# Moving part of the edge listing from VectorE to GpSimd in a two-layer graph attention kernel

## The chip, the core and the metric

The kernel runs on one core of a Trainium2 chip. The metric is the device time of one execution in microseconds. Three runs of the kernel before gave 1906.88, 1908.4 and 1909.48 us; the median, 1908.4 us, is the time that the prediction starts from. One more execution was recorded by the profiler (span 1902.5 us); all the rows below are from it.

## What is computed

Two graph attention layers over 3327 nodes with 1024 features, each followed by a residual and a normalisation. The adjacency matrix is sparse (each node has some 17 neighbours), symmetric, and has ones on its diagonal. Cut to what matters:

```python
h = (x @ W).reshape(C, H, D)                  # 8 heads of 128
e = alpha_src[:, :, None] + alpha_dst[:, None, :]
e = jnp.where(e >= 0, e, 0.2 * e)
e = jnp.where(adj[None] == 0, -jnp.inf, e)
out = jnp.einsum('hij,hjd->hid', softmax(e), h_heads)
x = layernorm(x + out)                        # layer 0
# layer 1: the same with one head, h = x @ W1, and a relu on the sum
```

## The kernel before

The 3327 rows are 26 tiles of 128 (the last one short). The kernel has two parts.

The **first part** does two jobs at the same time. It projects: `x @ W0` with 347 columns more or less at a time, three cuts of 8 matmuls for each tile (`project`, L475, TensorE row L479; `flip`, L470, transposes x first), and ScalarE brings the sums out of PSUM (`keep`, L485). And it lists edges: for each tile of 128 target rows, the columns of the ones in 128 x 3327 bytes of the adjacency matrix become a list of source rows, `idx`, and of targets, `tgt`. The **second part** (`sparse`, L741) fetches the listed rows by indirect DMA on the GpSimd queue, 17 for each tile and layer, and adds them up with matmuls. It can start only when the flag of L697 is read, for which the last list must have been counted and made.

The list of one tile t takes these steps (class `Edges`, L280 to L450):

- `words` (L301): GpSimd clears the diagonal (L308), ScalarE counts the ones of each row (L311, `junk`, the only large ScalarE step), VectorE folds the bytes into words (L318).
- `ends` and `ends2` (L324, L343): a matmul with a triangle of ones sums the counts up (L327, L346), ScalarE reads it (L328, L347), and GpSimd works out where each row's edges begin and end, in chains of seven and of five operations of one or two elements (L335 to L341, L348 to L353).
- `keys` and `columns` (L355, L364): VectorE finds up to 32 columns of each row by repeated search for the 8 largest (L274) and removal (L276); the result is `pack`, 128 x 32.
- `places` (L379): ScalarE takes the distance of each place from the middle of a row's stretch (L384 for 512 places, L385 for 128 more, `away`); a comparison with the row's count turns this into a 0/1 matrix `place` in bf16 (L391, L392). `pack` is split into a bf16 part and a bf16 remainder and put into `mv`, one of four buffers (L388, L389). `factors` (L291), called from `keep`, puts the exponentials of the source scores into the same kind of buffer on GpSimd (L296 to L299).
- `give` (L394): TensorE multiplies `place` by `mv` (L411, L401), which moves each row's columns to the places of its edges. `take` (L415): ScalarE reads the result out of PSUM into `xs` and others (L423 to L428).
- `sources` (L431): which of the 32 columns a place takes is an offset difference `kq` (L436, L437); an equality with 0 to 31, a product and a sum (L439 to L445) pick it, and `idx` is written (L450).

What sets the order is written out by hand. All engines take their instructions in the order of the program; `listing` (L506) is a generator of 7 steps for each tile, and `pace` (L537), called after every second matmul of the projection, takes the next step when it is due. In a round of it, the tile before (`old`) gives its places, the next tile (`new`) has its keys and columns searched, then come `take`, `count` of the tile four ahead, `sources` of the old tile, and `places` of the new one:

```python
                if old:
                    old.give(EB)
                    old.take()
                count(t + 4)
                yield
                if old:
                    old.sources()
                    yield
                while new and t + 1 not in scored:
                    yield
                if new:
                    new.places()
                    yield
```

The `while` sees to it that the factors of a tile are issued before its places. Since the projection and the list go at different rates, `keep`, with its four GpSimd operations and its ScalarE steps, falls in another place of the round from tile to tile.

Buffers: `pack`, `away`, `kq` and `xs` have one each, `place` has two, `mv` four.

Of the kernel before, what the change touches and what calls it, by code (L numbers as in the profile page):

```python
# [14 lines left out]
OP = mybir.AluOpType  # L15
# [4 lines left out]
P = 128  # L20
# [6 lines left out]
def kernel(  # L27
# [28 lines left out]
    nc = tc.nc  # L56
# [11 lines left out]
    KMAX = 32  # L68
    GT = 32
    NG = P // GT  # L70
    EB = 4
# [9 lines left out]
    NX = KMAX + 2 + H  # L81
    NY = NX + 2
    XO, XL = 1 + H, 2 + H
# [3 lines left out]
    def rows(t):  # L87
        return min(P, N - t * P)
# [68 lines left out]
    class Phase:  # L157
# [10 lines left out]
        def sbuf(self, tag, shape, bufs, name=None, dt=F32):  # L168
            return self.pool.tile(shape, dt, tag=tag, name=name or tag, bufs=bufs)
# [110 lines left out]
    class Edges:  # L280
# [83 lines left out]
        def columns(self, half):  # L364

            sbuf, ph = self.ph.sbuf, self.ph
            if half == 0:
                ki = sbuf("ki", [P, 2, KMAX], 1, dt=I32)
                nc.vector.tensor_copy(ki[:, 0, :], self.top)
                nc.vector.tensor_scalar(ki[:, 1, :], ki[:, 0, :], 511, None, op0=OP.bitwise_and)  # L370
                bits = sbuf("bits", [P, 8, KMAX], 1, dt=I32)
                nc.vector.tensor_tensor(bits, ki[:, 0:1, :].to_broadcast([P, 8, KMAX]), ph.bit, OP.bitwise_and)
                self.cols = sbuf("cols", [P, 8, KMAX], 1)
                nc.vector.tensor_tensor(self.cols, ki[:, 1:2, :].to_broadcast([P, 8, KMAX]), ph.base, OP.add)
                nc.vector.scalar_tensor_tensor(self.cols, bits, 0.0, self.cols, op0=OP.not_equal, op1=OP.mult)
                self.pack = sbuf("pack", [P, KMAX], 1)
            ph.largest(self.pack, self.cols.rearrange("p a b -> p (a b)"), half)

        def places(self):  # L379

            sbuf, ph, pack = self.ph.sbuf, self.ph, self.pack

            away = sbuf("away", [P, (EB + 1) * P], 1)
            nc.scalar.activation(away[:, : EB * P], ph.io_q, AF.Abs, bias=self.mid, scale=-1.0)  # L384
            nc.scalar.activation(away[:, EB * P :], ph.io_q[:, :P], AF.Abs, bias=self.mid2, scale=-1.0)  # L385

            mv = self.mv = ph.mvs[self.t % 4]
            nc.vector.tensor_copy(mv[:, 0, XL:NX], pack)  # L388
            nc.vector.tensor_tensor(mv[:, 1, XL:NX], pack, mv[:, 0, XL:NX], OP.subtract)  # L389
            self.place = sbuf("place", [P, (EB + 1) * P], 2, dt=BF16)  # L390
            nc.vector.tensor_scalar(self.place[:, : EB * P], away[:, : EB * P], self.deg, None, op0=OP.is_lt)  # L391
            nc.vector.tensor_scalar(self.place[:, EB * P :], away[:, EB * P :], self.more, None, op0=OP.is_lt)  # L392

        def give(self, b):  # L394

# [35 lines left out]
        def sources(self):  # L431

            sbuf, ph, t = self.ph.sbuf, self.ph, self.t
            xv, m = self.xs, NB - 1
            kq = sbuf("kq", [P, NB], 1)
            nc.vector.tensor_tensor(kq[:, :m], ph.io_k[:, :m], xv[:, :m, 0], OP.subtract)  # L436
            nc.vector.tensor_tensor(kq[:, m:], ph.io_k[:, m:], xv[:, m, KMAX + 1 :], OP.subtract)  # L437
            eq = sbuf("eq", [P, NB, KMAX], 1)
            nc.vector.tensor_tensor(  # L439
                eq, ph.io_l.unsqueeze(1).to_broadcast([P, NB, KMAX]),  # L440
                kq.unsqueeze(2).to_broadcast([P, NB, KMAX]), OP.is_equal,
            )
            nc.vector.tensor_tensor(eq, eq, xv[:, :, 1 : KMAX + 1], OP.mult)
            v = sbuf("v", [P, 2, NB], 1)
            nc.vector.tensor_reduce(v[:, 0, :], eq, AX.X, OP.add)  # L445

            nc.vector.tensor_scalar(
                v[:, 1, :], v[:, 0, :], 0.0, float(NONE if t > 1 else 1), op0=OP.is_equal, op1=OP.mult
            )
            nc.vector.scalar_tensor_tensor(idx[:, t, :], v[:, 0, :], -1.0, v[:, 1, :], op0=OP.add, op1=OP.add)  # L450


    with ExitStack() as own, tc.manual_schedule():
        ph = Phase(own, "proj", {"A": 2, "S": 1, "T": 2})
# [204 lines left out]
        for t in range(3, NT):  # L659
# [3 lines left out]
            if t == 12:  # L663
                n, own = NT - 1, pool.tile([P, NT], I32, bufs=1, name="own")
                nc.vector.memset(own[:, n:], 0)
                step, m = adj.ap[0][0] + 1, rows(n)
# [563 lines left out]
```

## Time and profile before

| Engine | busy, us | share of the span | instructions |
|---|---|---|---|
| TensorE matmul (PE) | 1502.7 | 79% | 14663 |
| TensorE weight load (PEld) | 887.9 | 47% | 14663 |
| VectorE (DVE) | 1146.0 | 60% | 3058 |
| ScalarE (ACT) | 546.5 | 29% | 1422 |
| GpSimd (POOL) | 1032.3 | 54% | 1391 |

GpSimd's time is nearly all in the second part, where it issues the fetches. In the first part it is busy for 12 or 13 us in 50. How the views are read: in the timeline, a row has the start and the length in us, the engine, the line of the program, what is written and read with its size, and in brackets the idle time before it and what ended that time. In the stretches, each engine's busy time is followed by the number of instructions. In the waits, a row gives the waiting engine and line, what it waited for, the total in us, the number of times, and the longest. In the groups, a row gives the busy time and the mean in ns, and after the next bar the idle time ahead of it. The ends of matmuls are modelled, so a TensorE that looks busy is not at its peak.

### The profile page before, as it was taken

Reading aid. Unit: us, or ns where it says so; the run is one execution under the profiler, and the core shown is the slowest. Engines: PE = TensorE matmul, PEld = TensorE weight load, DVE = VectorE, ACT = ScalarE, POOL = GpSimd, SP = SyncE. Lnnn points to the kernel's source line nnn. Section 1 sums busy time; section 2 is a strip of 40 time slices with the busy share of each in tenths; the row PEclk is TensorE's granted clock in tenths of the full one; section 3 lists DMA queues with packets and bytes.
Section 4 is the critical chain, followed back from the end, with each engine's and each line's share of the span. In section 5 each row is a group of like instructions: output and inputs, shape, how many; then the busy total and the mean of one; then the engine's idle time right before and its main releaser. Section 6 shows DMA issues by size and latency. Waiting matters only on the chain.

```text
span 1902.5 us, 38082 instructions
## 1 busy us (share of the span) xinstructions
PE 1502.7 (79%) x14663; PEld 887.9 (47%) x14663; DVE 1146.0 (60%) x3058; ACT 546.5 (29%) x1422; POOL 1032.3 (54%) x1391
## 2 busy tenths in 40 slices
PE   8699999999366556555556555399999999999997
PEld 5355555566254545445445444144444444444443
DVE  5799999987286666666666666344444444444442
ACT  5554544452123222222222222012222212222220
POOL 3322222220477666676666764577766667666650
PEclk9899999999678788888888888699999999999999
DMA  7656555421799999999999997899999999999980
GB/s 182 88 115 131 111 104 106 87 72 39 276 369 400 400 401 399 376 406 398 390 388 392 398 383 279 325 401 407 403 370 385 380 378 373 354 372 373 365 326 33
DMA packets 171068, 567.76 MB, mean 298 GB/s; under 512 B 27690, under 2 KB 34346, under 8 KB 170878
## 3 DMA queue, kind: packets, MB, share of 16 engines
q0 software_dynamic: 131056, 455.68, 67.2%
q1 hardware_dynamic: 39822, 109.56, 15.3%
q8 instruction: 118, 1.93, 0.4%
q14 instruction: 72, 0.59, 0.1%
HBM read 578.85 MB, written 42.97 MB: 327 GB/s over the span
## 4 chain that ended last, share of the span: by engine, by line
PE 50%; DMA 24%; DVE 12%; ACT 6%; issue 4%; POOL 3%; DVEq 0%; ACTq 0%; SPq 0%; POOLq 0%
DMA src<-h_d,idx 22%; PE mm L1023 20%; PE acc L991 12%; PE mm L479 11%; DVE e L868 3%; ACT junk L311 3%; PE acc L896 2%; PE tr L176 2%; POOL src L801 2%; DVE pr L929 1%; ACT xT L179 1%; DMA wt<-in_L_gnn_W_dram 1%; PE acc L880 1%; DVE top L274 1%; PE xp L411 1%
## 5 line engine op out<-in xcount | busy, mean ns | idle before, releaser
L801 POOL DMA_INDIRECT src<-h_d,idx x416 | 443.3, 1066 | 201.6 <-PE acc L896 52.3
L801 POOL DMA_INDIRECT src<-y_d,idx x416 | 415.4, 999 | 222.1 <-PE acc L991 89.4
L896 PE MATMUL acc<-src,e 128*32 128x128 f32 x6656 | 267.7, 328 | 260.0 <-DVE e L868 259.6
L479 PE MATMUL mm<-wt,xT 128*128 128x347 f32 (+1 forms) x1248 | 402.5, 468 | 3.1 <-DMA wt<-in_L_gnn_W_dram 2.5
L1023 PE MATMUL mm<-wt,xT 128*128 128x512 f32 x832 | 383.3, 604 | 0.8 <-DVE o L1026 0.8
L896 PEld LDWEIGHTS acc<-src,e 128*32 128x32 f32 x6656 | 226.3, 133 | 316.7 <-DVE e L868 290.7
L479 PEld LDWEIGHTS mm<-wt,xT 128*128 128x128 f32 x1248 | 228.2, 192 | 111.2 <-ACT ht L496 6.7
L1023 PEld LDWEIGHTS mm<-wt,xT 128*128 128x128 f32 x832 | 152.2, 190 | 199.5 <-issue 179.1
L991 PE MATMUL acc<-src,es 128*32 128x342 f32 (+1 forms) x2496 | 205.6, 463 | 33.8 <-DVE es L982 30.9
L868 DVE TENSOR_TENSOR e<-oh,way 128x1024 f32<-128x1024 f32 x130 | 158.8, 1221 | 60.6 <-ACT w L866 60.3
L991 PEld LDWEIGHTS acc<-src,es 128*32 128x32 f32 x2496 | 71.5, 111 | 158.8 <-issue 113.1
L866 ACT ACTIVATE w<-way 128x32 f32<-128x32 f32 (+1 forms) x130 | 24.7, 190 | 399.7 <-DVE way L864 388.3
L1026 DVE SCALAR_TENSOR_TENSOR o<-mm,y 128x512 f32<-128x512 f32 x52 | 36.0, 692 | 166.1 <-PE mm L1023 166.1
L1005 ACT ACTIVATE z<-y,ri 128x342 f32<-128x342 f32 (+1 forms) x78 | 39.5, 569 | 313.8 <-DVE ri L1001 313.8
L863 DVE TENSOR_TENSOR way<-src,re 128x32 f32<-128x32 f32 x104 | 20.9, 201 | 171.6 <-DMA src<-h_d,idx 153.2
L179 ACT ACTIVATE xT<-tr 128x512 f32<-128x512 f32 x104 | 59.3, 595 | 150.7 <-PE tr L176 150.7
L979 DVE TENSOR_TENSOR way<-way,src 128x128 f32<-128x128 f32 x104 | 31.1, 299 | 89.9 <-DMA src<-y_d,idx 44.4
L311 ACT ACTIVATE junk<-ad 128x3328 uint8<-128x3328 uint8 x26 | 78.3, 3013 | 16.1 <-POOL ad L308 16.1
L848 ACT ACTIVATE own<-own,es 128x128 f32<-128x128 f32 x208 | 63.6, 388 | 59.7 <-DVE es L845 59.7
L880 PE MATMUL acc<-end,e 128*128 128x128 f32 x416 | 63.0, 313 | 15.3 <-DVE e L868 15.3
L335 POOL TENSOR_TENSOR place_of<-cnt 128x1 f32<-128x1 f32 x26 | 5.0, 191 | 122.1 <-ACT cnt L328 102.5
L296 POOL CAST mvs<-r 128x8 bf16<-128x8 f32 x26 | 6.0, 231 | 118.2 <-ACT r L295 118.2
(188 smaller groups left out, 1953.7 us busy)
## 6 DMA issues: line engine op xcount, KB each, us to landing
h_d<-ht SPq DMA_DIRECT2D x26, 520.0 KB
own<-h_d SPq DMA_DIRECT2D x26, 520.0 KB
y_d<-y SPq DMA_DIRECT2D x26, 514.0 KB
y<-y_d SPq DMA_DIRECT2D x26, 514.0 KB
x<-in_x_dram SPq DMA_DIRECT2D x25, 512.0 KB
y<-in_x_dram SPq DMA_DIRECT2D x25, 512.0 KB
out_dram<-o SPq DMA_DIRECT2D x25, 512.0 KB
ad<-in_adj_dram POOLq DMA_DIRECT2D x25, 415.9 KB
```

The lines of the kernel that those rows point to most:

```text
L176: nc.tensor.transpose(tr[:, k, :], src[:, (4 * g + k) * P : (4 * g + k + 1) * P], ident)
L179: nc.scalar.activation(part, tr, AF.Copy)
L311: nc.scalar.activation(junk, ad, AF.Copy, accum_out=self.deg)
L479: nc.tensor.matmul(acc, xT[t][:, k, :], wt[:, k, CUTS0[c] : CUTS0[c + 1]], start=k == 0, stop=k == KT - 1)
L801: nc.gpsimd.indirect_dma_start(out=s[:, g, :w], out_offset=None, in_=table[:, :], in_offset=bass.IndirectOffsetOnAxis(ap=idx[:, t, b * NG ...
L848: nc.scalar.activation(hn, hn, AF.Copy, scale=es[:, n : n + 1])
L868: nc.vector.tensor_tensor(e, oh.unsqueeze(2).to_broadcast([P, ng, H, wide]), wp.unsqueeze(3).to_broadcast([P, ng, H, wide]), OP.mult,)
L880: nc.tensor.matmul(self.acc[h // 4][:, h % 4, :], e[:, 0, h, :], rowsof[:, 0, h, :], start=False, stop=h % 4 == 3,)
L896: nc.tensor.matmul(self.acc[h // 4][g * GT : (g + 1) * GT, h % 4, :], e[:, g, h, :], rowsof[:, g, h, :], start=first and h % 4 == 0, stop= ...
L991: nc.tensor.matmul(self.acc[c][to, :m], es[:, g, :], s[:, g, CUTS[c] : CUTS[c + 1]], start=b == 0, stop=b == EB,)
L1005: nc.scalar.activation(z[:, cut], self.res[:, cut], AF.Copy, scale=ri[:, 1:2])
L1023: nc.tensor.matmul(acc, xT[:, k, :], wt1[:, k, half], start=k == 0, stop=k == KT - 1)
```

## The change

Six operations for each tile go from VectorE's queue to GpSimd's: the two comparisons that make `place`, the two copies that split `pack`, and the two differences that make `kq`. `pack` gets a second buffer, so that VectorE can write the next tile's columns while GpSimd still reads this one's. It is meant to take work off VectorE, which is nearly always busy in the first part. The order of the program stays as it is on TensorE, ScalarE and the DMA queue of SyncE; the instructions leave one queue and stand at the same point of the program in another.

```diff
@@ columns
-                self.pack = sbuf("pack", [P, KMAX], 1)
+                self.pack = sbuf("pack", [P, KMAX], 2)
@@ places
-            nc.vector.tensor_copy(mv[:, 0, XL:NX], pack)
-            nc.vector.tensor_tensor(mv[:, 1, XL:NX], pack, mv[:, 0, XL:NX], OP.subtract)
+            nc.gpsimd.tensor_copy(mv[:, 0, XL:NX], pack)
+            nc.gpsimd.tensor_tensor(mv[:, 1, XL:NX], pack, mv[:, 0, XL:NX], OP.subtract)
             self.place = sbuf("place", [P, (EB + 1) * P], 2, dt=BF16)
-            nc.vector.tensor_scalar(self.place[:, : EB * P], away[:, : EB * P], self.deg, None, op0=OP.is_lt)
-            nc.vector.tensor_scalar(self.place[:, EB * P :], away[:, EB * P :], self.more, None, op0=OP.is_lt)
+            nc.gpsimd.tensor_scalar(self.place[:, : EB * P], away[:, : EB * P], self.deg, None, op0=OP.is_lt)
+            nc.gpsimd.tensor_scalar(self.place[:, EB * P :], away[:, EB * P :], self.more, None, op0=OP.is_lt)
@@ sources
-            nc.vector.tensor_tensor(kq[:, :m], ph.io_k[:, :m], xv[:, :m, 0], OP.subtract)
-            nc.vector.tensor_tensor(kq[:, m:], ph.io_k[:, m:], xv[:, m, KMAX + 1 :], OP.subtract)
+            nc.gpsimd.tensor_tensor(kq[:, :m], ph.io_k[:, :m], xv[:, :m, 0], OP.subtract)
+            nc.gpsimd.tensor_tensor(kq[:, m:], ph.io_k[:, m:], xv[:, m, KMAX + 1 :], OP.subtract)
```

In GpSimd's queue the two copies stand directly ahead of the two comparisons. In front of them stand, in the order of the program, the diagonal and the mask's DMA issue of `count`, then `kq`, and in some rounds the four factors of `keep`; behind them come the chains of `ends` and `ends2`.

## The prediction

> **What bounds the kernel now.** The page's 40 slices show two parts. In the first 10 slices (to about 488 us) DMA moves 39 to 182 GB/s, against some 400 later, and TensorE is at 9 tenths or more from slice 3 on; this is where the edges are listed and x@W0 is projected, and it is the only part that the diff touches. The second part begins at the flag (L697, 486 us), whose value needs the last list. So what counts is when the first part ends. Second view, busy time by stretch:
>
> ```profile
> core 0: us, PE busy (x) PEld busy (x) DVE busy (x) ACT busy (x) POOL busy (x), PEclk, DMA share, GB/s
> 111.00:160.00 49.00, 46.37 (x316) 28.32 (x314) 43.62 (x125) 24.50 (x66) 11.92 (x54) 1.00 0.60 130
> 160.00:190.00 30.00, 29.78 (x202) 18.21 (x202) 28.28 (x81) 14.57 (x41) 7.95 (x36) 1.00 0.62 126
> 190.00:300.00 110.00, 105.66 (x728) 65.10 (x727) 100.05 (x282) 55.27 (x148) 26.46 (x122) 1.00 0.54 108
> 408.00:481.00 73.00, 73.00 (x495) 44.57 (x494) 54.65 (x152) 22.11 (x74) 8.72 (x42) 1.00 0.11 41
> ```
>
> VectorE (DVE) is 89 to 94% busy, which invites unloading it. But TensorE is 95 to 100% busy, and its own work (624 projection matmuls, the flips, the places) is unchanged: the part can shorten only by TensorE's idle time. Third view, the waits, TensorE in 78:481 and VectorE in 100:440:
>
> ```profile
> PE xp L411 <- DVE place L391: 20.6, 15, 9.7
> DVE place L391 <- ACT away L384: 11.4, 17, 1.5
> ```
>
> TensorE's idle time is the wait of the first L411 of a list for `place`; 9.7 of the 20.6 us is list 0 (TensorE starved at 68 to 78 us while ScalarE counts three masks). So 10.9 us is the most that could be won later. And in 17 of 22 lists VectorE itself stood waiting for ScalarE's `away`. Fourth view, the timeline of list 20:
>
> ```profile
> 385.71 0.22 PE L401 MATMUL xp<-mvs,place 128*128 128x43 bf16 x3
> 386.92 3.02 ACT L311 ACTIVATE junk<-ad 128x3328 uint8<-128x3328 uint8 x1
> 390.36 0.21 ACT L295 ACTIVATE r<-sd 128x8 f32<-128x8 f32 x1
> 390.59 0.45 ACT L496 ACTIVATE ht<-mm 128x330 f32<-128x330 f32 x1
> 390.92 0.73 ACT L384 ACTIVATE away<-io_q,place_of 128x512 f32<-128x512 f32 x1
> 391.46 0.21 POOL L299 TENSOR_TENSOR mvs<-r,mvs 128x8 bf16<-128x8 f32 x1
> 391.68 0.49 DVE L391 TENSOR_SCALAR place<-away,cnt 128x512 bf16<-128x512 f32 x1 [0.68 <-ACT away L384]
> 392.23 0.24 PE L411 MATMUL xp<-mvs,place 32*128 32x42 bf16 x12 [0.36 <-DVE place L391]
> ```
>
> The loop is TensorE (L401 of the list before) -> ScalarE (xs, the 3.02 us count, ht, away) -> place -> TensorE. `place` starts 0.03 us after `away` ends; VectorE's load is not in it. Setting `away`, `place` and L411 side by side for the 26 lists: `place` was late because of VectorE only in lists 6, 7, 15, 16 and 18. List 15:
>
> ```profile
> 313.13 0.71 ACT L384 ACTIVATE away<-io_q,place_of 128x512 f32<-128x512 f32 x1
> 314.76 0.48 DVE L391 TENSOR_SCALAR place<-away,cnt 128x512 bf16<-128x512 f32 x1
> 315.30 0.24 PE L411 MATMUL xp<-mvs,place 32*128 32x42 bf16 x12 [0.76 <-DVE place L391]
> ```
>
> [...] The trace [...] has no one-input compare. [...] GpSimd's L348 takes 0.19 us 21 times and 0.40 to 0.42 us five times.
>
> **The change, part by part.** It takes off VectorE per list, from these rows (100:440): 0.179 + 0.192 + 0.516 + 0.280 + 0.181 + 0.152 = 1.50 us of some 14.2 us, 39 us in all:
>
> ```profile
> L391 DVE TENSOR_SCALAR place<-away,cnt 128x512 bf16<-128x512 f32 x22 | 11.4, 516 | 11.4 <-ACT away L384 11.4
> L392 DVE TENSOR_SCALAR place<-away,place_of 128x128 bf16<-128x128 f32 x21 | 5.9, 280 | 0.0
> L389 DVE TENSOR_TENSOR mvs<-pack,mvs 128x32 bf16<-128x32 f32 x22 | 4.2, 192 | 0.8
> L576 POOL TENSOR_TENSOR pr<-wt,av 128x1024 f32<-128x1024 f32 x6 | 14.2, 2364 | 18.4 <-DMA wt<-in_L_gnn_W_dram 8.1 <-ACT junk_h L585 7.1 <-issue 3.3
> L308 POOL TENSOR_SCALAR_AFFINE_SELECT ad<-ad 128x128 int8<-128x128 int8 x26 | 7.6, 294 | 0.0
> ```
>
> *The compare L391 on GpSimd* is the disputed cost. Lower end: a one-element operation takes 0.20 us (L338) and L308 0.29 us for 128, so 0.7 ns an element and 0.20 + 512 x 0.7 = 0.57 us. Upper end: the two-input slope of L576, (2.36 - 0.19)/1024 = 2.1 ns, gives 1.27 us. I take 0.75 us[...]. GpSimd starts some 0.07 us after ScalarE (L296 after L295) against 0.03 us for VectorE, so `place` comes D = 0.75 - 0.49 + 0.05 = 0.31 us later after `away`. L392 (about 0.3 us) is needed only by the last group, 7 us on: nothing.
>
> *The two copies L388/L389 on GpSimd* stand ahead of the compare in its queue; 0.2 us each, 0.27 us from start to start. They wait for `pack`, ready 4 us earlier. Where the queue is otherwise empty they cost nothing, ScalarE's count hides them. But in lists 2, 11 and 20 to 25 the order puts the factors L296 to L299 directly ahead, and those start only after ScalarE's r. L299 starts at 391.46 in list 20, so L388 at 391.6, L389 at 391.9 and the compare at 392.06 instead of 391.68: 0.4 us more. In list 1 the chain L348 to L353 is ahead as well (L353 started at 97.66, 97.2 without VectorE's interference), so the compare starts at about 97.75, not 96.34: 1.4 us more.
>
> *kq on GpSimd* (L436/L437) waits for xs behind L308 and the mask's DMA issue (0.6 us); it is done by 387.3 in list 20, VectorE finishes the words at 387.7: hidden, and behind kq only the copies wait. *Second buffer of pack*: lets VectorE write the next list's columns while GpSimd reads; it removes a wait that would be new. *VectorE* has nothing on the path any more; its next wait is for kq.
>
> Sum of added TensorE waits. Lists whose place already was the last to arrive, with an empty GpSimd queue (0, 4, 5, 8, 10, 12, 13, 17, 19): 9 x 0.31 = 2.8; lists 3 and 14, which had 0.05 us to spare, 0.5 together; list 18, of which VectorE had 0.1: 0.2. Lists 2, 11, 20, 24, 25: 5 x 0.71 less 0.12 us to spare in each of the last two = 3.3; lists 21 to 23 have the room (0.8, 0.1 and 1.4 us). List 1: 1.65. Lists 15 and 16 gain, since `away` was done 0.9 and 0.6 us before VectorE came: -0.6 and -0.3. Lists 6, 7 and 9: nothing. Tail: the last kq is on the direct path from xs to the flag, two GpSimd steps and two hops for VectorE's 0.3 us: 0.2. Total 2.8 + 0.5 + 0.2 + 3.3 + 1.65 - 0.9 + 0.2 = 7.75 us. Each counts fully, because all that follows, ScalarE's chain included, hangs on TensorE. So 1908.4 + 7.8 = 1916.2 us.
>
> **Rivals.** *It cancels.* A compare of 0.57 us, D = 0.13, takes 0.18 us from some 20 lists, -3.5; without the 0.4 us of the copies (if GpSimd takes them faster) -2 more: +2, 1910 us. For: L308's slope. Against: list 1 and the hops stay. *Faster.* If VectorE's backlog, not ScalarE, feeds the waits (the chain of waits does run through VectorE at 160 to 190 and 300 to 330 us), 1.5 us less a list removes most of the 10.9 us: about -8, 1900 us. Against: even in those stretches TensorE is 97 to 99% busy, and ScalarE's order holds nothing that VectorE makes. [...] If the compare takes 1.27 us, 20 x 0.5 = +10 more; or if VectorE's two-input operations (0.57 to 0.73 us) block it half the time, 18 x 0.35 = +6: about 1924 us. Against: when `away` ends, VectorE should be in the one-tensor searches L274/L276, where it stays 5 us.
>
> **How the numbers follow.** Forecast 0.50, contention or a slow compare 0.16, cancelling 0.19, faster 0.15. The range 1903 to 1926 takes in the two middle cases and most of the slow one, and leaves out most of the fast one. Slower by over 0.2% (3.8 us): nearly all of the forecast and the slow case, 0.63; within 0.2%: 0.22; faster: 0.15.
>
> **What would show it.** L391 on GpSimd at 0.75 us; VectorE's busy time down 39 us with TensorE's unchanged; the wait of L411 for place up from 20.6 us to about 28, longest growth in lists 1, 2, 11, 20; second part unchanged. Wrong if L411's waits shrink, if `away` itself comes earlier after L401, or if the compare shows 1 us and more.

## The result, and the profile after

The changed kernel takes 1960.84 us (median of four runs, 1957.84 to 1962.83), the one before 1907.64 us in the same comparison: a ratio of 1.0277, 95% interval 1.0259 to 1.0294, 53 us slower. I had forecast 1916.2 us, slower by 8, with a range up to 1926.

The difference lies where the change is. In the profiled runs the flag that ends the first part is written at 486.3 us before and at 540.5 us after, 54.1 us later; the rest of the span is 1416.1 and 1419.9 us. The busy times by stretch of the changed kernel, over the lists (columns as before: busy us of each engine, and PEclk, TensorE's granted clock):

```profile
111.00:170.00 59.00, 53.38 (x350) 32.84 (x349) 41.63 (x107) 26.09 (x74) 24.49 (x83) 0.97 0.52 109
170.00:300.00 130.00, 114.71 (x737) 69.65 (x735) 96.07 (x245) 57.62 (x152) 51.23 (x164) 0.95 0.52 103
300.00:454.00 154.00, 138.90 (x926) 85.23 (x926) 119.29 (x306) 69.92 (x190) 66.11 (x210) 0.97 0.41 83
454.00:540.00 86.00, 75.65 (x506) 45.96 (x504) 51.70 (x135) 25.09 (x87) 24.62 (x76) 0.99 0.12 43
```

VectorE was relieved: in the first three stretches it is 71 to 77% busy, where it was at 89 to 94%. TensorE, which was at 95 to 100%, is at 88 to 90%, and its clock, 1.00 throughout in these stretches before, is not full any more. The waits of TensorE after, from list 0 on:

```profile
PE xp L411 <- POOL place L391: 56.6, 26, 11.3
```

This was 20.6 us in 15 lists; it is now 56.6 us in all 26. The timeline of list 20, to be laid beside that of before:

```profile
430.39 0.22 PE L401 MATMUL xp<-mvs,place 128*128 128x43 bf16 x3
431.64 3.02 ACT L311 ACTIVATE junk<-ad 128x3328 uint8<-128x3328 uint8 x1
435.65 0.73 ACT L384 ACTIVATE away<-io_q,place_of 128x512 f32<-128x512 f32 x1
436.18 0.21 POOL L299 TENSOR_TENSOR mvs<-r,mvs 128x8 bf16<-128x8 f32 x1
436.62 0.24 POOL L389 TENSOR_TENSOR mvs<-pack,mvs 128x32 bf16<-128x32 f32 x1
436.84 1.58 POOL L391 TENSOR_SCALAR place<-away,cnt 128x512 bf16<-128x512 f32 x1
438.48 0.24 PE L411 MATMUL xp<-mvs,place 32*128 32x42 bf16 x12 [1.93 <-POOL place L391]
```

From L401 to the end of `away` it takes 5.94 us before and 5.99 us after: ScalarE's chain is what it was. From the end of `away` to the start of the comparison it takes 0.46 us instead of 0.03 (the factors and the two copies go first), and the comparison takes 1.58 us instead of 0.49. The wait grows from 0.36 to 1.93 us. The groups:

```profile
L391 POOL TENSOR_SCALAR place<-away,cnt 128x512 bf16<-128x512 f32 x26 | 43.0, 1654 | 48.5 <-ACT away L384 48.5
L392 POOL TENSOR_SCALAR place<-away,place_of 128x128 bf16<-128x128 f32 x26 | 15.9, 613 | 0.0
L389 POOL TENSOR_TENSOR mvs<-pack,mvs 128x32 bf16<-128x32 f32 x26 | 13.4, 514 | 2.1
```

The one large comparison has a mean of 1654 ns, more than twice the 0.75 us that I had assumed, and above the 1.27 us that I had called the upper end.

Two questions are left by this. The waits grew by 36.0 us, the first part by 54.1: where are the other 18? And how much is due to the comparison, how much to the order of GpSimd's queue?

### The profile page after: what moved, and what is told of

It is laid out like the page before. It is cut to its first block, busy times and chain, and to the rows that moved or that the text cites. A ratio compares the mean times of both kernels' runs of the same rounds, so it can differ in the third digit from the quotient of the medians.

```text
span 1960.4 us, 38076 instructions
## 1 busy us (share of the span) xinstructions
PE 1532.9 (78%) x14663; PEld 907.8 (46%) x14663; DVE 1118.6 (57%) x2902; ACT 546.2 (28%) x1422; POOL 1120.0 (57%) x1547
## 4 chain that ended last, share of the span: by engine, by line
PE 50%; DMA 22%; DVE 9%; ACT 8%; POOL 6%; issue 4%; DVEq 0%; POOLq 0%; ACTq 0%; SPq 0%
PE mm L1023 19%; DMA src<-h_d,idx 18%; PE acc L991 12%; PE mm L479 11%; ACT junk L311 4%; DVE e L868 3%; PE acc L896 2%; PE tr L176 2%; POOL place L391 2%; POOL src L801 2%; DVE pr L929 1%; ACT xT L179 1%; DMA wt<-in_L_gnn_W_dram 1%; PE acc L880 1%; DMA src<-y_d,idx 1%
## 5 line engine op out<-in xcount | busy, mean ns | idle before, releaser
L896 PE MATMUL acc<-src,e 128*32 128x128 f32 x6656 | 280.9, 339 | 252.9 <-DVE e L868 252.8
L479 PE MATMUL mm<-wt,xT 128*128 128x347 f32 (+1 forms) x1248 | 418.5, 483 | 3.9 <-DMA wt<-in_L_gnn_W_dram 3.3
L896 PEld LDWEIGHTS acc<-src,e 128*32 128x32 f32 x6656 | 236.6, 137 | 312.2 <-DVE e L868 285.0
L479 PEld LDWEIGHTS mm<-wt,xT 128*128 128x128 f32 x1248 | 236.4, 199 | 118.2 <-issue 14.6
L1023 PEld LDWEIGHTS mm<-wt,xT 128*128 128x128 f32 x832 | 151.6, 189 | 198.4 <-issue 178.0
L979 DVE TENSOR_TENSOR way<-way,src 128x128 f32<-128x128 f32 x104 | 31.1, 299 | 90.4 <-ACT way L949 44.4
L391 POOL TENSOR_SCALAR place<-away,cnt 128x512 bf16<-128x512 f32 x26 | 43.0, 1654 | 48.5 <-ACT away L384 48.5
L888 PE MATMUL acc<-own,ident 128*128 128x512 f32 x104 | 62.3, 683 | 9.8 <-ACT own L848 8.6
```

The lines of the kernel that those rows point to most:

```text
L391: nc.gpsimd.tensor_scalar(self.place[:, : EB * P], away[:, : EB * P], self.deg, None, op0=OP.is_lt)
L479: nc.tensor.matmul(acc, xT[t][:, k, :], wt[:, k, CUTS0[c] : CUTS0[c + 1]], start=k == 0, stop=k == KT - 1)
L888: nc.tensor.matmul(self.acc[b - 1].rearrange("p h d -> p (h d)"), ident, self.h[:, (b - 1) * HALF : b * HALF], start=False, stop=False,)
L896: nc.tensor.matmul(self.acc[h // 4][g * GT : (g + 1) * GT, h % 4, :], e[:, g, h, :], rowsof[:, g, h, :], start=first and h % 4 == 0, stop= ...
L1023: nc.tensor.matmul(acc, xT[:, k, :], wt1[:, k, half], start=k == 0, stop=k == KT - 1)
```

## The experiments

The runs were made in three groups; each kernel is compared with the kernel before in its own group (1910.6 us for e1 to e4, 1964.7 us for e5 to e8, 1907.7 us for e9 to e11). Besides the time I use the moment of the flag, since the slower group's extra time lies in the second part (from the flag to the end it takes 1471.8 us in e6 and 1416.1 us in the profile of before). For each kernel I have that moment from one profile only.

**e1, only the comparison.** `nc.gpsimd` for L391 alone, all else as before.

> Only L391, the large comparison, goes to GpSimd; the small one, both copies and kq stay on VectorE. Length theory (the comparison takes 1.57 us instead of 0.49 and starts 0.07 us later, on the loop TensorE - ScalarE - place - TensorE): about 1.15 us more in the 14 lists that already waited, 0.2 to 0.9 us in six others, some 20 us, and some 8 us more if the clock falls as it does in the changed kernel: 1928 to 1938 us. Queue theory (what hurts is what stands ahead of the moved operations in GpSimd's queue, and kq): nearly nothing, under 1915 us.

Measured: 1942.73 us, ratio 1.0178 (1.0148 to 1.0208), flag at 517.4 us, 31.1 later. The comparison takes 1.574 us in nearly every list, and as a rule starts 0.1 us after `away`:

```profile
L391 POOL TENSOR_SCALAR place<-away,cnt x26: 1560/1574/1655, 79.6 to 502.1; 128x512 bf16<-128x512 f32 x26
  PEld L411: 61.1, 26
  PE xp L411: 46.8, 25
```

These are the lowest, median and highest ns, and who waited for it. TensorE's wait is 26.2 us over that of before. One operation of six makes more than half of the loss, and the queue theory (under 1915 us) falls as the sole cause. The time is nearly 5 us above the length theory's range: that had counted some 20 us of waits, and list 1 alone, where the chain L348 to L353 stands ahead of the comparison, lost 2.5 us.

**e2, all but the comparison.**

```diff
-            nc.gpsimd.tensor_scalar(self.place[:, : EB * P], away[:, : EB * P], self.deg, None, op0=OP.is_lt)
+            nc.vector.tensor_scalar(self.place[:, : EB * P], away[:, : EB * P], self.deg, None, op0=OP.is_lt)
```

> The whole change but L391, which stays on VectorE. Length theory alone: no cost is left, 1.0 us of work a list is off VectorE, 1905 to 1908 us. Queue theory: in lists 9, 10 and 19 the factors L296 to L299 stand ahead of kq, so that VectorE gets to place some 2.9 us later; list 1 has the chain L348 to L353 ahead of the copies (0.7 us); six lists wait 0.2 us for the copies: 1915 to 1921 us.

Measured: 1926.56 us, ratio 1.0083 (1.0053 to 1.0113), flag at 506.7 us, 20.4 later. So the other five operations cost, too, though each takes less time than the comparison and none of their results looked urgent. The length theory alone falls as well. TensorE's waits for the lists grow by 9.2 us, nearly all of it in lists 9, 10 and 19, as the queue theory has it; but the time is 6 us above that theory's range as well.

**e3, only kq.** L436 and L437 on GpSimd, all else as before.

> Only kq (L436, L437) goes to GpSimd. Queue theory: lists 9, 10 and 19 wait for kq behind the factors and lose some 2.9 us each, 1914 to 1919 us. If kq is hidden, as I had predicted: 1907 to 1909 us.

Measured: 1924.70 us, ratio 1.0087 (1.0057 to 1.0117), flag 14.8 us later. TensorE's wait grows by 9.7 us, and nearly all of it in three lists: 2.99, 3.71 and 3.98 us in lists 9, 10 and 19, which had 0, 0.37 and 0.36 before. List 19 of e3:

```profile
385.20 0.21 POOL L299 TENSOR_TENSOR mvs<-r,mvs 128x8 bf16<-128x8 f32 x1
385.36 0.23 POOL L436 TENSOR_TENSOR kq<-io_k,xs 128x16 f32<-128x16 f32 x1
385.76 0.73 DVE L439 TENSOR_TENSOR eq<-io_l,kq 128x544 f32<-128x544 f32 x1 [4.47 <-POOL kq L437]
388.73 0.48 DVE L391 TENSOR_SCALAR place<-away,cnt 128x512 bf16<-128x512 f32 x1
389.27 0.25 PE L411 MATMUL xp<-mvs,place 32*128 32x42 bf16 x12 [3.98 <-DVE place L391]
```

In these lists the four factors stand ahead of kq in GpSimd's queue, and they wait for ScalarE, which is at its 3 us count. VectorE idles 4.47 us for a result of 17 numbers, then has its five operations on the sources to do, and only then reaches `place`. The three waits grew by 3.0 to 3.6 us, about as expected (2.9); the time is 6 to 11 us over the expectation, some 2 us of which are the group's. The next experiment explains a part of the rest.

**e4, keeping TensorE busy.** The changed kernel, with two matmuls of no use ahead of the first L411 of a list (their result is overwritten by `give`):

```diff
                 self.xp = self.ph.bank("S", [P, NG, HALF], "xp")
+                for _ in range(2):
+                    nc.tensor.matmul(self.xp[:, 0, :347], ident, wt[:, 0, :347], start=True, stop=True)
```

> The changed kernel with two float32 matmuls of 128x347 (about 1.2 us) that compute nothing of use, issued by TensorE into xp directly ahead of the first L411 of each list, where it waits 2.2 us on average; give overwrites their result. Clock theory (the half-speed stretches at 116 to 454 us follow from these waits and cost about 16 us): those stretches go, L479 falls from 418 us to about 403 us busy, 1944 to 1950 us. If the clock has another cause: the matmuls fit into the waits and the time stays at 1958 to 1964 us, or rises.

Measured: 1951.41 us, ratio 1.0221 (1.0193 to 1.0249) against the changed kernel's 1.0277, flag at 531.0 us instead of 540.5. That is 1.4 us above the clock theory's range and 6.6 us below the other's. More work on TensorE makes it faster:

```profile
111.00:170.00 59.00, 56.88 (x372) 35.63 (x371) 42.87 (x108) 27.31 (x74) 24.55 (x83) 1.00 0.54 111
170.00:300.00 130.00, 120.75 (x799) 74.08 (x799) 100.71 (x259) 57.92 (x159) 55.50 (x174) 1.00 0.52 107
300.00:454.00 154.00, 149.57 (x990) 92.70 (x989) 122.36 (x316) 70.60 (x190) 67.16 (x216) 1.00 0.40 79
```

The clock is full again from 111 us on as the two digits show it (one half-speed record of nine is left), and L479 is busy for 407.3 us instead of 418.5 (402.5 before). So the second loss is TensorE's clock: at nine of the twelve waits of 1.9 to 4.0 us that lists 1 to 25 of the changed kernel have, its profile records half the clock for 3.4 us. List 9 shows it, the weight loads (PEld, 0.19 us and 0.29 us apart in the median) with gaps between them, 0.58 us apart:

```profile
244.01 0.24 PE L411 MATMUL xp<-mvs,place 32*128 32x42 bf16 x12 [2.49 <-POOL place L391]
244.18 3.26 PE L479 MATMUL mm<-wt,xT 128*128 128x347 f32 x7
246.07 0.34 PEld L479 LDWEIGHTS mm<-wt,xT 128*128 128x128 f32 x1 [0.24 <-issue]
```

Each of the nine records is 3.41 us long and begins between 0.2 us before and 1.7 us after the end of the wait. The length of a wait alone doesn't tell whether the clock falls: in the changed kernel 1.93 us (list 20) and 1.96 us (list 12) came with a fall, 2.30 us (list 8) and 1.95 us (list 18) without one.

**e5, the operation by itself.** Sixteen GpSimd operations ahead of everything else. VectorE is idle beside the first eight, but for the last of them, and busy beside the second eight.

> The kernel before with 16 additional GpSimd operations at its very start, on tiles of their own, whose results nobody reads: twice in turn the comparison as in L391 (512 elements, a row's count as the scalar, bf16 out), the same on 128, the same with float32 out, the same with a constant as the scalar, a product with a constant, a copy to bf16, a copy to float32, and a two-input difference, all of 512 but the second. If every one-input operation with arithmetic costs 2.5 ns an element here, all four are at 1.4 to 1.6 us and only the copies are below. If it is the bf16 output: float32 out takes 0.6 to 0.8 us. If it is the scalar from memory: the constant takes 0.6 to 0.8 us. If L391 was only held up by VectorE: all take 0.6 to 0.8 us here, where VectorE is nearly idle. Two inputs by L576's slope: 1.27 us.

Measured (groups of GpSimd, whole lines):

```profile
L553 POOL TENSOR_SCALAR q_bf<-q_in,q_w 128x512 bf16<-128x512 f32 x2 | 3.1, 1574 | 0.1
L555 POOL TENSOR_SCALAR q_out<-q_in,q_w 128x512 f32<-128x512 f32 x2 | 3.1, 1567 | 0.0
L556 POOL TENSOR_SCALAR q_out<-q_in 128x512 f32<-128x512 f32 x2 | 3.0, 1487 | 0.2
L557 POOL TENSOR_SCALAR q_out<-q_in 128x512 f32<-128x512 f32 x2 | 3.0, 1498 | 0.2
L560 POOL TENSOR_TENSOR q_out<-q_in,q_w 128x512 f32<-128x512 f32 x2 | 2.5, 1274 | 0.2
L558 POOL CAST q_bf<-q_in 128x512 bf16<-128x512 f32 x2 | 1.2, 609 | 0.0
```

L553 is the comparison of L391; L555 has float32 out, L556 a constant for the scalar, L557 a product. All take 1.49 to 1.57 us on average, and the first and the second of each kind differ by 0.03 us at most. It is neither the type, nor the scalar, nor the comparison, nor VectorE: a one-input operation with arithmetic is slow on GpSimd, slower than a two-input one, which is where the slope of L576 put it (1.27 us). Only the copies take 0.61 us.

**e6, kq back on VectorE, the rest of the change kept.**

> The changed kernel with kq back on VectorE. Queue theory: lists 9, 10 and 19 lose the part of their wait that comes from VectorE's two-input operations running late and holding up the copy and the comparison (0.5 us for the comparison, 0.4 for L389), some 1 us each, the tail gains 0.2 us, and one or two falls of the clock may go: 1952 to 1958 us. If kq's delay of some 3 us came in full beside the comparison's, as it does in e3: 1944 to 1948 us.

Measured: ratio 1.0195 (1.0153 to 1.0238), in the slower group; flag at 534.8 us, 5.7 before that of the changed kernel, which is the smaller of the two forecasts (3 to 9 us); by the ratio it would be some 6 to 23 us, which takes in both. The waits of lists 9, 10 and 19 are 1.40, 2.07 and 2.07 us instead of 2.49, 3.19 and 3.46. So kq's delay and the comparison's do not add up in full: with place on GpSimd, VectorE's late work is off the path, and kq costs 1.1 to 1.4 us in these lists, by what follows it. In list 9 the comparison starts 1.19 us after `away` in the changed kernel and 0.64 us after it in e6, and it takes 2.12 us instead of 1.58. VectorE's L443, with two inputs, starts 0.02 us after the long one; L439, of the same kind, ran beside the copy L389, which took 0.63 us; in e6 both had been done. It is so in all lists of the changed kernel: L389 takes 0.63 to 0.78 us in the 16 lists where it runs beside L439, and 0.24 us in the other ten; the comparison takes 2.03 to 2.12 us in the four lists where it runs beside L443 or beside L372 to L375, and 1.56 to 1.58 us in the other 22. Why, the profile doesn't show.

**e7, the count moved; nothing on GpSimd.** The kernel before, with the count of the tile four ahead taken from between `take` and `places` to the third step:

```diff
+                    if s == 2 and old:
+                        count(t + 4)
                     yield
                 if old:
                     old.give(EB)
                     old.take()
-                count(t + 4)
+                else:
+                    count(t + 4)
```

> The kernel before with only the place of count in the order changed: the count of the tile four ahead (L308, L311, L318) is issued after the third step of a round instead of after take, so that ScalarE's 3.0 us count no longer stands between xs and away. Path theory (ScalarE's chain, not VectorE's load, makes place late): the waits of L411 after list 0 fall from 10.9 us to 3 us or less, 1897 to 1902 us on a chip where before takes 1908. If VectorE's load makes it late: no change, 1905 to 1911 us.

Measured: ratio 0.9999 (0.9981 to 1.0017), flag at 484.5 us. The time is what VectorE's theory forecast, but its reason is refuted by the waits of TensorE:

```profile
PE xp L411 <- DVE place L391: 10.5, 3, 9.7
PE op L346 <- ACT xT L179: 4.2, 3, 1.7
PE tr L176 <- ACT cnt L328: 3.0, 1, 3.0
PE tr L176 <- ACT cnt L347: 2.4, 3, 1.0
```

The waits for `place` are gone but for list 0, with VectorE loaded as before. In their place stand waits for ScalarE to empty the two small PSUM banks, 8.9 us more than before: the count is one piece of 3 us, and in both places something behind it on ScalarE is late.

**e8, the changed kernel with the count moved.**

> The changed kernel with the same move of count as in e7. Path theory: away comes some 3.4 us earlier after L401, which is more than the 1.15 us that the comparison on GpSimd adds, so most of the 36 us of added waits go and the clock stays up: 1900 to 1915 us. Lists 9, 10 and 19, where kq stands behind the factors, keep a part. If the cost lay in GpSimd's total work or in its disturbing VectorE: still over 1940 us.

Measured: ratio 1.0088 (1.0065 to 1.0112), some 17 us over before, which would be some 1925 us and so misses both ranges; flag 17.7 us later. The waits of L411 fall from 56.6 to 23.4 us (2.8 over before), so most of the comparison is hidden, as forecast; but the banks' waits of e7 come in (7.2 us over before), and the clock's loss is still 6.8 us over before, all of it ahead of 111 us. The expectation had left both out.

**e9 to e11, the count in pieces.** The kernel before, with four counts of 832 columns, one for each step (e9), two of 1664 (e10), and e9 with the two copies on GpSimd and the second `pack` (e11). The edit of e9, cut to what matters:

```diff
+                        if s == 0:
+                            lists[t + 4].clear(ads[t + 4])
+                        lists[t + 4].part(ads[t + 4], junk, s)
                     yield
                 if old:
                     old.give(EB)
                     old.take()
-                count(t + 4)
+                    lists[t + 4].add()
+                    lists[t + 4].fold(ads.pop(t + 4))
```

> The kernel before with the count of the tile four ahead cut into four counts of 832 columns, one in each of the four steps of a round, and their sum taken after take; the diagonal is cleared in the first step; VectorE's fold of the words stays where it was. Some 1.5 us more of work on ScalarE a list, but no single piece over about 1 us. Path theory: the waits of L411 after list 0 (10.9 us before) fall under 3 us without the waits for a PSUM bank that the whole count made in e7 (9 us); the flag comes at 478 to 482 us instead of 486, ratio 0.995 to 0.998. If VectorE's 15.05 us a list is then the bound, or the pieces still hold up the banks: flag at 484 to 488 us, ratio 0.999 to 1.002.

> As e9, but in two counts of 1664 columns, in the second and the fourth step. Path theory: pieces of 1.6 us hold up a bank now and then, so between e7 (flag 484.5 us) and e9: 481 to 484 us. If the length of a piece doesn't matter: as e9.

> e9, and beside it the two copies L388 and L389 on GpSimd with the second buffer of pack: the part of the change that costs GpSimd no more than VectorE. If VectorE's load bounds e9, 0.37 us less a list gives up to 5 us: flag 2 to 5 us before that of e9. If TensorE bounds it: within 1 us of e9, and up to 2 us later where the factors stand ahead of the copies.

Measured: e9 1897.76 us, ratio 0.9949 (0.9934 to 0.9965), flag 479.9; e10 1898.62 us, 0.9959 (0.9943 to 0.9975), flag 477.7; e11 1896.07 us, 0.9940 (0.9924 to 0.9955), flag 478.4. All three beat both kernels, by some 9 to 12 us against before. The path theory's range holds for e9's flag. Halves do as well as quarters: pieces of 1.58 us cost no more here than pieces of 0.89 us. In e9 VectorE still came late in five lists, 2.3 us together. In e11 it doesn't (list 1 waits 0.4 us for the copy instead), and from 111 to 470 us TensorE never stops; two stretches of it:

```profile
111.00:160.00 49.00, 49.00 (x326) 30.48 (x325) 44.78 (x121) 28.01 (x95) 15.39 (x63) 1.00 0.67 127
300.00:470.00 170.00, 170.00 (x1145) 105.05 (x1145) 145.73 (x395) 79.56 (x276) 42.95 (x179) 1.00 0.32 71
```

So VectorE's load was worth some 1.5 us of flag, once ScalarE's chain was out of the way, less than the forecast 2 to 5 us; the waits show the gain, while the times of e9 and e11 alone don't, since their intervals overlap.

**The sum.** For each kernel: how much later the flag comes than before; the growth of TensorE's waits for L411; the growth of what half speed cost (half of its recorded length up to the flag); and what else TensorE did or waited for.

| Kernel | flag, us | waits L411 | half speed | else | sum |
|---|---|---|---|---|---|
| e3, kq | +14.8 | +9.7 | +3.4 | | 13.1 |
| e2, all but the comparison | +20.4 | +9.2 | +10.2 | | 19.4 |
| e1, the comparison | +31.1 | +26.2 | +5.1 | | 31.3 |
| the change | +54.1 | +36.0 | +18.8 | | 54.8 |
| e4, with idle matmuls | +44.7 | +8.5 | +5.1 | +30.7, those matmuls | 44.3 |
| e7, count moved | -1.8 | -10.1 | -1.7 | +8.9, banks | -2.9 |
| e11, quarters, copies | -7.9 | -10.5 | +3.4 | | -7.1 |

(30.7 us: 104 matmul records at the spacing of L479, 7.09 us for 24.) The terms account for every row within 2 us. A flag from one profile isn't surer than some 4 us: ahead of list 0 all these kernels do the same work, and yet its `away` starts at 76.9 us before, at 79.0 us in the changed kernel and at 76.8 to 80.8 us in the others. Some of the half speed is of that time, too (1.7 of the 18.8 us). Counted from that `away` on, the change makes the flag 52.0 us later, and the terms give 53.1; e9, e10 and e11 make it 10.2, 10.5 and 11.8 us earlier.

## Why the prediction was wrong, step by step

- **What bounds the kernel** was read rightly: the loop TensorE, ScalarE, `place`, not VectorE's load. All of the change's waits lie there, and e7 and e9 removed most of those of the kernel before without unloading VectorE. (The page's first ten slices end at 475.6 us, not at about 488; nothing hangs on it.)
- **The comparison on GpSimd** is the step that failed most. The 0.75 us that I had taken lies between my two ends (0.57 us by the slope of L308, 1.27 us by that of L576) and was a guess: no row of before showed such a comparison on GpSimd. Measured are 1.57 us, and 1.65 us on average within the whole change. Only copies came under 0.75 us here (0.61 us). My upper end, the two-input slope, was no bound: e5 has the one-input operation slower than the two-input one. With D = 1.15 instead of 0.31 us, terms of some 5 us became the 26.2 us of e1. A comparison of 1 us and more was one of my signs of being wrong, and it came.
- **The clock** was missing. I counted an added wait at its length ("each counts fully"); in the changed kernel 18.8 us at half speed came to the 36.0 us of added waits. The trace of before had the sign: after the 9.7 us wait of list 0 the weight loads of L479 took 0.34 us instead of 0.19.
- **kq hidden** was wrong for lists 9, 10 and 19. I had followed it in list 20 and generalised; the factors' place in GpSimd's queue moves from list to list, and I had used that order for the copies but not for kq. Alone it costs 9.7 us of waits (e3), within the whole change 1.1 to 1.4 us in each of three lists (e6).
- **The copies** cost 0.36 us in list 20 as forecast (0.4), where the factors stand ahead; the hop from ScalarE was 0.10 us instead of 0.07. **List 1** lost 2.5 us instead of 1.65; the excess is the longer comparison's. It lost as much in e1, where the copies stayed on VectorE: what stands ahead there is the chain, not the copies.
- **Lists 15 and 16**, forecast to gain 0.6 and 0.3 us, lost 0.3 and 0.7, since the comparison took more than VectorE's lateness. In e2, where it stayed on VectorE, their waits did go. **The tail** was right: from the last L411 to the flag 13.95 instead of 13.72 us.
- **The rivals.** "Faster" and "it cancels" fall. "Contention or a slow compare" came nearest, and was put at too small a size by the false upper end and by the clock.

## What to carry to other kernels

Moving work off a busy engine pays only if that engine's lateness ends a wait: here VectorE itself waited for `away` in 17 of 22 lists, and a count of 3 us on ScalarE, half idle in this part, was the cause. Before an operation changes its engine, its cost there needs a row of the same kind of operation, and its place in the new queue has to be followed in every order that occurs, since what stands behind a waiting instruction waits with it: VectorE's 4.47 us in list 19 of e3 are of this kind. And a wait of TensorE can cost more than its length: here 36.0 us of added waits came with 18.8 us at half speed.

## What the runs showed of the hardware that I had not expected

- On GpSimd a one-input operation with a scalar, 128x512 in float32, takes 1.49 to 1.57 us, be it a comparison or a product, with a constant or a row's scalar, into bf16 or float32; a two-input difference takes 1.27 us, a copy or a cast 0.61 us.
- TensorE's clock fell to half for 3.4 us at nine of the changed kernel's twelve waits of 1.9 to 4.0 us, and two matmuls of no use ahead of each list's first L411 brought the flag 9.4 us forward (ratio 1.0221 instead of 1.0277).
